# Moving normalisations, a bias and copies from VectorE to ScalarE and GpSimd in a twelve-sublayer perceiver kernel

## The chip, the core and the metric

The kernel runs on one core of one Trainium2 chip. The core has five engines that are spoken of here: TensorE (PE: matmuls, transposes, and its weight loads, PEld), VectorE (DVE), ScalarE (ACT), GpSimd (POOL), and the DMA queues that SyncE (SP) issues. Each engine carries out its own instructions in the order in which they stand in the built program, and waits for the others where data or buffers require it. The metric is device time in microseconds.

## The reference, cut to what matters

The model applies twelve residual sublayers to x of shape (128, 32, 128): four layers L0 to L3 of an xattn, an attn and an ffn each. Every sublayer reads a layer norm of x:

```python
x = x + _L1_xattn_ref(_layernorm(x), ctx_2048, ...)   # rmsnorm, one product, a depooled context
x = x + _L1_attn_ref(_layernorm(x), ...)              # a state-space block
x = x + _L1_ffn_ref(_layernorm(x), ...)               # 4 of 16 experts
x = x + _L2_xattn_ref(_layernorm(x), ctx_2048, ...)   # attention over 257 + 32 keys, 16 heads
x = x + _L2_attn_ref(_layernorm(x), ...)              # an RWKV recurrence and its channel mix
```

An expert of L1_ffn computes `min(h, 7) * sigmoid(1.702 * min(h, 7)) * 8` from `h = W1 x + b1`, then a second product. All arithmetic is in float32.

## The kernel before, in words

The 4096 tokens lie in SBUF as eight groups X[0] to X[7] of four tiles, each of 128 tokens by 128 channels. A layer runs group by group, and neighbouring layers are pipelined against each other:

- L0_xattn and then L0_ffn come first. The L1 layer of groups 0 and 1 runs as a side job in small steps between the experts of L0_ffn.
- `middle` (line 865) has nine iterations. Iteration `it` runs L2_xattn of group it, L1 (xattn13, L1_attn, L1_ffn) of group it + 2 and L2_attn of group it - 1. `abreast` interleaves the three by their steps: 20, 27 and 16. L1 takes part in iterations 0 to 5. Iterations 6 and 7 have L2_xattn and L2_attn alone, iteration 8 only the last L2_attn.
- L2_ffn follows, and then L3, in which xattn13 (line 947, shared by L1 and L3), L3_attn and L3_ffn run abreast.

The program does not fix an order for the engines except where `follow` does so: a scheduler of the framework takes the instructions as they are recorded and decides for each engine in which order they stand. Tiles come from pools; a tile with `bufs=2` has two buffers, and a new one waits until the old one has been read.

*Norms.* `stats` (line 189) computes mean and variance on DVE and takes the inverse root on POOL (line 215). `normed` (line 218) then applies (x - mean) * rs to each of four tiles on DVE (line 221). `normed_act` (line 1588), so far used only by L3_attn and L3_ffn, computes nb = -mean * rs on DVE (line 1592) and then rs * x + nb on ACT (line 1595). The result goes to `transposed` (line 228, PE) and from there into the first product.

*The experts of L1_ffn* (from line 1085). Each of 16 experts has a product ph (line 1087), DVE adds the bias and takes the minimum with 7 (line 1089, u), ACT takes a tanh (line 1091, s), DVE combines (line 1092, s), PE makes the second product py (line 1095), and four DVE instructions add it to X with the routing weight (line 827). PSUM tiles ph and py come from one pool of two buffers; u and s have two buffers each.

*L2_xattn.* A step handles one batch entry: POOL masks the query (QM, line 238, three buffers), PE makes four score tiles S (line 1180, two PSUM buffers), DVE takes the negated maximum nm (line 1181), ACT the exponential E (line 1182), PE transposes E in three key parts (line 1191, two PSUM buffers), these are copied to ET, the first and third part by ACT (line 1196) and the second by DVE (line 1194), and PE multiplies them with the values (line 1208), which ACT copies to OU (line 1209).

*L2_attn* has a norm of X twice over (xl and xn) and one of xl later on; kk (line 1298, POOL), xT, kv and exponentials on ACT, scans on DVE.

Of the kernel before, what the change touches and what calls it, by code (L numbers as in the profile page):

```python
# [9 lines left out]
FP = mybir.dt.float32  # L10
I32 = mybir.dt.int32
U32 = mybir.dt.uint32
AF = mybir.ActivationFunctionType
ALU = mybir.AluOpType
# [151 lines left out]
class Kern:  # L166
# [780 lines left out]
    def xattn13(self, g, w, hs, hps):  # L947
        nc = self.nc
        Dg = hs.tile([128, 4, 128], FP, tag="Dg")
        nc.sync.dma_start(Dg, self.dd[g * 512:(g + 1) * 512, :].rearrange("(i p) c -> p i c", p=128))  # L950
        mv, rs, s2 = self.stats(hs, self.X[g], 4, 1e-5, 1e-5)
        xn = self.normed(hs, self.X[g], mv, s2)
        pt = hps.tile([128, 512], FP, tag="m", name="pxt")
        self.transposed(pt, xn)
        xT = hs.tile([128, 512], FP, tag="xT")
        nc.scalar.activation(xT, pt, AF.Copy, scale=w["gres"])
        yield 1
        ps = hps.tile([128, 4, 128], FP, tag="m", name="ph")
        for i in range(4):
            nc.tensor.matmul(ps[:, i, :], lhsT=xT[:, i * 128:(i + 1) * 128], rhs=w["w"], start=True, stop=True)  # L960
        nc.gpsimd.tensor_tensor(Dg, Dg, w["ginit"].unsqueeze(1).to_broadcast([128, 4, 128]), ALU.mult)
        nc.gpsimd.tensor_tensor(Dg, Dg, w["b"].unsqueeze(1).to_broadcast([128, 4, 128]), ALU.add)
        nc.gpsimd.tensor_tensor(self.X[g], self.X[g], Dg, ALU.add)  # L963
        self.addx(g, ps.rearrange("p i c -> p (i c)"))
        yield 1
# [15 lines left out]
    def L1_attn(self, g, w, consts, ms, mps):  # L981
        nc = self.nc
        av, A, hw = consts
        wi = w["wi"].rearrange("p (k f) -> p k f", k=4)
        cw = hw[:, 0:8].rearrange("p (k j) -> p k j", k=2)
        dw, Bw, Cw = (w[n].rearrange("p (k s) -> p k s", k=2) for n in ("dw", "Bw", "Cw"))
        wo = w["wo"].rearrange("p (k d) -> p k d", k=2)
        mv, rs = self.stats(ms, self.X[g], 4, 1e-5)
        xn = self.normed(ms, self.X[g], mv, rs)
        ps = mps.tile([128, 512], FP, tag="m", name="pxt")  # L990
        self.transposed(ps, xn)
        xT = ms.tile([128, 512], FP, tag="xT")
        nc.scalar.copy(xT, ps)
        yield 1
        XC = ms.tile([128, 2, 16, T], FP, tag="XC")
        SG = ms.tile([128, 2, 512], FP, tag="SG")
        for k in range(2):
            ps = mps.tile([128, 16, T], FP, tag="m", name="pin")
            nc.tensor.matmul(ps, lhsT=wi[:, k, :], rhs=xT, start=True, stop=True)
            xc = XC[:, k]  # L1000
            nc.scalar.activation(xc, ps, AF.Identity, bias=hw[:, 8 + k:9 + k], scale=cw[:, k, 3:4])
            for j in (1, 2, 3):
                nc.vector.scalar_tensor_tensor(xc[:, :, j:], ps[:, :, :T - j], cw[:, k, 3 - j:4 - j], xc[:, :, j:], ALU.mult, ALU.add)
            yield 1
        XCf = XC.rearrange("p k b t -> p (k b t)")
        XS = ms.tile([128, 1024], FP, tag="XS")
        nc.scalar.activation(XS, XCf, AF.Tanh)
        nc.vector.scalar_tensor_tensor(XCf, XS, 1.0, XCf, ALU.add, ALU.mult)
        for k in range(2):
            ps = mps.tile([128, 512], FP, tag="m", name="pgt")  # L1010
            nc.tensor.matmul(ps, lhsT=wi[:, 2 + k, :], rhs=xT, start=True, stop=True)
            nc.scalar.activation(SG[:, k, :], ps, AF.Tanh, scale=0.5)
            nc.vector.scalar_tensor_tensor(SG[:, k, :], SG[:, k, :], 1.0, ps, ALU.add, ALU.mult)
        pd = mps.tile([128, 512], FP, tag="m", name="pd")
        for k in range(2):
            for j, lw in enumerate((dw[:, k, :], Bw[:, k, :], Cw[:, k, :], av)):
                nc.tensor.matmul(pd[32 * j:32 * j + 16], lhsT=lw, rhs=XC[:, k], start=k == 0, stop=k == 1)
        pB, pC, pX = pd[32:48], pd[64:80], pd[96:112]
        yield 1

        ze = ms.tile([128, 2, 512], FP, tag="XS", name="ze")
        z, e = ze[0:16, 0], ze[0:16, 1]
        nc.vector.tensor_scalar(z, pd[0:16], w["db"], None, ALU.add)
        nc.vector.scalar_tensor_tensor(e, z, -1.0, z, ALU.mult, ALU.min)
        nc.scalar.activation(e, e, AF.Exp)
        nc.scalar.activation(e, e, AF.Ln, bias=1.0)
        dt = z
        nc.vector.scalar_tensor_tensor(dt, z, 0.0, e, ALU.max, ALU.add)
        a = ms.tile([128, 16, T], FP, tag="xl", name="aa")[0:16]
        nc.scalar.activation(a.rearrange("p b t -> p (b t)"), dt, AF.Exp, scale=A)  # L1030
        nc.vector.memset(a[:, :, 0:1], 0.0)
        bx = ms.tile([128, 512], FP, tag="Dg", name="bx")[0:16]
        nc.vector.tensor_tensor(bx, dt, pX, ALU.mult)
        nc.vector.tensor_tensor(bx, bx, pB, ALU.mult)
        h = e
        nc.vector.tensor_tensor_scan(h, a.rearrange("p b t -> p (b t)"), bx, 0.0, ALU.mult, ALU.add)
        nc.vector.scalar_tensor_tensor(h, h, 0.5, pC, ALU.mult, ALU.mult)
        yield 1
        py = mps.tile([128, 512], FP, tag="m", name="py")
        nc.tensor.matmul(py, lhsT=self.ones[0:16, :], rhs=h, start=True, stop=True)  # L1040
        for k in range(2):
            nc.vector.tensor_tensor(SG[:, k, :], SG[:, k, :], py, ALU.mult)
            nc.vector.scalar_tensor_tensor(SG[:, k, :], XC[:, k].rearrange("p b t -> p (b t)"), w["D"][:, k:k + 1], SG[:, k, :], ALU.mult, ALU.add)
        po = mps.tile([128, 4, 128], FP, tag="m", name="po")
        for i in range(4):
            for k in range(2):
                nc.tensor.matmul(po[:, i, :], lhsT=SG[:, k, i * 128:(i + 1) * 128], rhs=wo[:, k, :], start=k == 0, stop=k == 1)
        self.addx(g, po.rearrange("p i c -> p (i c)"))
        yield 1
# [3 lines left out]
    def L1_ffn(self, g, w, gs, gps):  # L1053
        nc = self.nc
        w1 = w["w1"].rearrange("p (e i) -> p e i", e=16)
        w2 = w["w2"].rearrange("p (e d) -> p e d", e=16)
        mv, rs, s2 = self.stats(gs, self.X[g], 4, 1e-5, 1e-5)
        xn = self.normed(gs, self.X[g], mv, s2)
        ps = gps.tile([128, 512], FP, tag="m", name="pxt")
        self.transposed(ps, xn)  # L1060
        xT = gs.tile([128, 512], FP, tag="xT")
        nc.scalar.activation(xT, ps, AF.Copy, scale=w["sc"])
        yield 1
        xl = self.normed(gs, self.X[g], mv, rs, tag="xl")
        nc.gpsimd.tensor_tensor(self.X[g], self.X[g], xl, ALU.add)
        ps = gps.tile([128, 4, 16], FP, tag="m", name="plg")
        for i in range(4):
# [14 lines left out]
        self.addx(g, ps.rearrange("p i c -> p (i c)"))  # L1082
        nc.vector.tensor_scalar(R, R, 4.0, None, ALU.mult)
        yield 1
        for e in range(16):
            ps = gps.tile([128, 512], FP, tag="m", name="ph")
            nc.tensor.matmul(ps, lhsT=w1[:, e, :], rhs=xT, start=True, stop=True)
            u = gs.tile([128, 512], FP, tag="gu", bufs=2, name="u")
            nc.vector.tensor_scalar(u, ps, w["b1"][:, e:e + 1], 7.0, ALU.add, ALU.min)
            s = gs.tile([128, 512], FP, tag="gsw", bufs=2, name="s")  # L1090
            nc.scalar.activation(s, u, AF.Tanh, scale=0.851)
            nc.vector.scalar_tensor_tensor(s, s, 1.0, u, ALU.add, ALU.mult)
            py = gps.tile([128, 4, 128], FP, tag="m", name="py")
            for i in range(4):
                nc.tensor.matmul(py[:, i, :], lhsT=s[:, i * 128:(i + 1) * 128], rhs=w2[:, e, :], start=True, stop=True)
            self.add_weighted(self.X[g], py, R[:, :, e:e + 1])
            yield 1


# [10 lines left out]
    def L2_xattn(self, g, w, WP, e32, ys, yc, yx, yps, ypt, ypq):  # L1110
        nc = self.nc
        mv, rs = self.stats(ys, self.X[g], 4, 1e-5)
        xn = self.normed(ys, self.X[g], mv, rs)
        nc.gpsimd.tensor_tensor(self.X[g], self.X[g], w["bp"].unsqueeze(1).to_broadcast([128, 4, 128]), ALU.add)
        ps = ypq.tile([128, 512], FP, tag="q", name="pxt")
        self.transposed(ps, xn)
# [67 lines left out]
    def L2_xattn_transposes(self, st, t, b, cs, yx, ypt):  # L1184
        nc, E = self.nc, t["E"][b]
        for c in cs:
# [3 lines left out]
            for j in range(4):  # L1190
                self.follow(st, nc.tensor.transpose(pt[0:n, j * 128:(j + 1) * 128], E[:, j, k0:k1], self.ident))  # L1191
            ET = yx.tile([128, 512], FP, tag=f"ET{c}", name="ET")
            if c == 1:
                nc.vector.tensor_copy(ET[0:n], pt[0:n])  # L1194
            else:
                nc.scalar.copy(ET[0:n], pt[0:n])
            t["ET"][b].append(ET)

    def L2_xattn_values(self, st, t, b, yc, ypq):
# [41 lines left out]
    def L2_attn(self, g, w, wd, wt, wv, rs_, rpa):  # L1241
        nc = self.nc
        Wfv = wv.rearrange("p (k d) -> p k d", k=4)
        mv, rs, s2 = self.stats(rs_, self.X[g], 4, 1e-5, 1e-5)
        xl = self.normed(rs_, self.X[g], mv, rs, tag="xl")
        xn = self.normed(rs_, self.X[g], mv, s2)
        yield 1
        o = []
        for way in range(2):
# [33 lines left out]
        yield 1  # L1283

        mv, rs = self.stats(rs_, xl, 4, 1e-5)
        xn = self.normed(rs_, xl, mv, rs)
        ps = rpa.tile([128, 512], FP, tag="r", name="pxt2")
        self.transposed(ps, xn)
        xT = rs_.tile([128, 512], FP, tag="xT", name="xT2")
# [436 lines left out]
```

## Time and profile before

| what | us |
|---|---|
| median of 3 runs | 5026.24 (5025.77 to 5035.71) |
| the profiled execution | 5026.48 |
| its span, first to last instruction | 5024.7 |
| L1 of groups 0 and 1 beside L0_ffn | about 2200 to 2832 |
| iterations 0 to 5 of `middle` (with L1) | about 2832 to 3888 |
| iterations 6 and 7 | about 3888 to 4107 |
| last L2_attn | about 4107 to 4190 |
| L3 | about 4684 to the end |

The bounds are the first and last starts of the lines named: S of L2_xattn runs from 2832.5 to 4107.8, ph of L1_ffn ends at 3888, the first norm of L3_attn starts at 4684. The mean granted TensorE clock is 0.928 of full speed. A row of waits reads "engine, what it wanted to do, <- who released it: us in all, times, longest". A row of one line's instructions gives least, median and greatest duration in ns. Busy time of PE is that of pipelined matmuls, so a full row is not the peak of the engine.

### The profile page before, as it was taken

What the parts mean: (1) busy time and instruction counts of PE and PEld (TensorE: products, weight loads), DVE (VectorE), ACT (ScalarE), POOL (GpSimd) and SP (SyncE); (2) the same over time, 40 slices, a digit from 0 to 9 for tenths busy, and PEclk for the clock granted to TensorE, in tenths of its full rate; (3) what the DMA queues carried; (4) which work ended last, traced back from release to release, by engine and by line L of the source; (5) the groups of instructions that cost most, each with busy time, mean ns of one, the idle gap of its engine ahead of it and who ended that gap; (6) DMA issues with size and microseconds to landing.
All of it is one profiled execution on the core that took longest, in us unless ns stands there. A gap on an engine that the chain in (4) does not pass through costs nothing. (4 is left out here: it accounts for less than half of the span.)

```text
span 5024.7 us, 91248 instructions
## 1 busy us (share of the span) xinstructions
PE 4396.5 (87%) x34654; PEld 3147.0 (63%) x34654; DVE 3445.9 (69%) x10361; ACT 2388.4 (48%) x6481; POOL 1068.1 (21%) x1065
## 2 busy tenths in 40 slices
PE   7999898989898898879999888898888886879688
PEld 5777676767666676657766556565556653546455
DVE  5334959585867768582856689888888775777444
ACT  4555444454444445434444445454454554773233
POOL 1011111111111102121010122322322332322443
PEclk9999999999999999989999999999899987999677
DMA  4223141312222131323000001101010110000100
GB/s 138 61 60 56 43 67 38 63 47 56 47 54 53 49 60 41 51 74 40 1 12 3 27 27 28 28 26 29 25 28 28 37 42 19 1 1 14 38 13 11
DMA packets 354344, 193.27 MB, mean 38 GB/s; under 512 B 180065, under 2 KB 336481, under 8 KB 353265
## 3 DMA queue, kind: packets, MB, share of 16 engines
q1 hardware_dynamic: 353906, 187.45, 16.0%
q8 instruction: 273, 4.47, 0.4%
q14 instruction: 165, 1.35, 0.1%
HBM read 156.43 MB, written 30.96 MB: 37 GB/s over the span
## 5 line engine op out<-in xcount | busy, mean ns | idle before, releaser
L215 POOL TENSOR_TENSOR rs<-ve,w_const 128x4 f32<-128x4 f32 (+1 forms) x192 | 194.0, 1011 | 1706.2 <-DVE ve L213 1627.9
L541 PE MATMUL S<-cT,q 128*128 128x257 f32 x2048 | 535.4, 401 | 21.3 <-ACT E L545 21.0
L541 PEld LDWEIGHTS S<-cT,q 128*128 128x128 f32 x2048 | 386.6, 198 | 145.5 <-issue 57.8
L543 DVE TENSOR_REDUCE nm<-S 128x1 f32<-128x257 f32 x512 | 214.9, 420 | 367.5 <-PE S L541 365.7
L545 ACT ACTIVATE E<-S,nm 128x257 f32<-128x257 f32 x512 | 242.8, 475 | 362.3 <-DVE nm L544 361.3
L1180 PE MATMUL S<-cT,QM 128*128 128x289 f32 x1024 | 316.0, 427 | 74.7 <-ACT E L1182 69.8
L827 DVE SCALAR_TENSOR_TENSOR X<-py,R,X 128x128 f32<-128x128 f32 x768 | 223.6, 343 | 155.7 <-PE py L820 83.1
L1182 ACT ACTIVATE E<-S,nm 128x289 f32<-128x289 f32 x512 | 252.8, 498 | 153.6 <-DVE nm L1181 144.8
L820 PEld LDWEIGHTS py<-w_L_ffn,Hh 128*128 128x128 f32 x2048 | 259.6, 198 | 62.8 <-issue 40.3
L719 DVE TENSOR_TENSOR A<-A,elt 128x400 f32<-128x400 f32 (+22 forms) x608 | 295.6, 486 | 4.8
L524 PE MATMUL pq<-xT,WQK 128*128 128x128 f32 x2048 | 259.8, 284 | 36.1 <-ACT q L525 35.6
L717 DVE TENSOR_TENSOR elt<-A,row 128x400 f32<-128x400 f32 (+22 forms) x608 | 285.6, 470 | 8.0 <-DVE row L711 0.2
L580 PE MATMUL po<-TA,cN 128*128 128x512 f32 x512 | 274.9, 620 | 0.8 <-ACT TA L569 0.8
L1180 PEld LDWEIGHTS S<-cT,QM 128*128 128x128 f32 x1024 | 175.7, 194 | 158.5 <-issue 49.9
L524 PEld LDWEIGHTS pq<-xT,WQK 128*128 128x128 f32 x2048 | 244.8, 195 | 47.4 <-ACT q L525 43.7
L816 ACT ACTIVATE Hh<-pu,w_L_ffn 128x512 f32<-128x512 f32 x256 | 173.4, 686 | 212.6 <-PE pu L815 203.9
L820 PE MATMUL py<-w_L_ffn,Hh 128*128 128x128 f32 x2048 | 268.6, 284 | 3.7 <-ACT Hh L816 3.6
L581 PE MATMUL po<-TB,cN 128*128 128x512 f32 x512 | 267.6, 605 | 1.4 <-DVE TB L570 1.4
L555 ACT ACTIVATE E<-E,sm 128x256 f32<-128x256 f32 x512 | 218.4, 497 | 74.5 <-DVE sm L551 63.0
L815 PE MATMUL pu<-xT,w_L_ffn 128*128 128x512 f32 x512 | 247.6, 606 | 0.0
L1191 PE MATMUL pt<-w_const,E 128*96 128x128 f32 (+1 forms) x1536 | 233.2, 286 | 2.2 <-DVE ET L1194 1.9
L594 PE MATMUL pout<-WVO,OT 128*128 128x128 f32 x2048 | 234.2, 275 | 0.3 <-ACT OT L582 0.3
(471 smaller groups left out, 10204.7 us busy)
## 6 DMA issues: line engine op xcount, KB each, us to landing
cT<-ctxT SPq DMA_DIRECT2D x128, 257.0 KB
cN<-ctx SPq DMA_DIRECT2D x128, 256.0 KB
cT<-ctxT SPq DMA_DIRECT2D x32, 514.0 KB
phik<-PW SPq DMA_DIRECT2D x32, 256.0 KB
phiq<-P SPq DMA_DIRECT2D x32, 256.0 KB
A<-phik SPq DMA_DIRECT2D x128, 64.0 KB
PQ<-phiq SPq DMA_DIRECT2D x32, 256.0 KB
cN<-ctx SPq DMA_DIRECT2D x32, 194.0 KB
```

The costliest lines, as they stand in the source:

```text
L524: self.follow(st, nc.tensor.matmul(ps[:, k, :, :], lhsT=WQK[:, 4 * j + k, cb * 128:(cb + 1) * 128], rhs=t["x"], start=True, stop=True))
L541: self.follow(st, nc.tensor.matmul(S, lhsT=t["QP"][j][:, cb, b, :, :], rhs=t["cT"][b][:, cb, :], start=cb == 0, stop=cb == 1))
L545: nc.scalar.activation(E[:, j, 0:LK], S, AF.Exp, bias=m, accum_out=sm[:, j:j + 1])
L580: self.follow(st, nc.tensor.matmul(po, lhsT=cN[:, 0, c], rhs=TA, start=True, stop=False), nc.tensor.matmul(po, lhsT=cN[:, 1, c], rhs=TB, s ...
L581: nc.tensor.matmul(po, lhsT=cN[:, 1, c], rhs=TB, start=False, stop=True))
L594: self.follow(st, nc.tensor.matmul(po[:, 0, :], lhsT=OT[:, cb, h, :, :], rhs=WVO[:, cb, h, :], start=h == 0 and cb == 0, stop=False))
L717: nc.vector.tensor_tensor(t, A[:, k, :, i0:i1].rearrange("p h i -> p i h").unsqueeze(3).to_broadcast([128, m, HC, n]), row[:, :, i0:N].uns ...
L719: nc.vector.tensor_tensor(A[:, i0:i1, :, i0:N], A[:, i0:i1, :, i0:N], t, ALU.subtract)
L815: nc.tensor.matmul(ps, lhsT=wu[:, e, k * 128:(k + 1) * 128], rhs=xT[:, q, :], start=True, stop=True)
L820: nc.tensor.matmul(py[:, i, :], lhsT=Hh[k][:, i * 128:(i + 1) * 128], rhs=wd[:, e, k, :], start=k == 0, stop=k == 3)
L1180: self.follow(st, nc.tensor.matmul(S, lhsT=t["QM"][:, 0, 4 * j:4 * j + 4, :], rhs=t["cT"][:, b, :], start=True, stop=True))
L1182: nc.scalar.activation(E[:, j, :], S, AF.Exp, bias=nm[:, j:j + 1], accum_out=sm[:, j, b:b + 1])
```

## The change

Eight calls of `normed` become `normed_act`: in xattn13, in L1_attn, twice in L1_ffn, in L2_xattn, and three times in L2_attn. (xattn13's one call serves L1 and L3.) In L1_ffn the bias is added by ACT in reading ph out of PSUM, the minimum is taken in place by POOL, and the second product of an expert is recorded after the first product of the next, so that the loop has 17 steps. In L2_xattn the second transposed part is copied by ACT too. In the changed file the lines up to 1085 keep their numbers; bias, minimum, second product and tanh stand at 1091, 1092, 1097 and 1101, and what follows the loop stands seven lines further on, and four lines further on from the edit of the copies onward.

```diff
-        xn = self.normed(hs, self.X[g], mv, s2)
+        xn = self.normed_act(hs, self.X[g], mv, s2, "xn")
...
-        for e in range(16):
-            ps = gps.tile([128, 512], FP, tag="m", name="ph")
-            nc.tensor.matmul(ps, lhsT=w1[:, e, :], rhs=xT, start=True, stop=True)
-            u = gs.tile([128, 512], FP, tag="gu", bufs=2, name="u")
-            nc.vector.tensor_scalar(u, ps, w["b1"][:, e:e + 1], 7.0, ALU.add, ALU.min)
-            s = gs.tile([128, 512], FP, tag="gsw", bufs=2, name="s")
-            nc.scalar.activation(s, u, AF.Tanh, scale=0.851)
-            nc.vector.scalar_tensor_tensor(s, s, 1.0, u, ALU.add, ALU.mult)
-            py = gps.tile([128, 4, 128], FP, tag="m", name="py")
-            for i in range(4):
-                nc.tensor.matmul(py[:, i, :], lhsT=s[:, i * 128:(i + 1) * 128], rhs=w2[:, e, :], start=True, stop=True)
-            self.add_weighted(self.X[g], py, R[:, :, e:e + 1])
+        S = {}
+        for e in range(17):
+            if e < 16:
+                ps = gps.tile([128, 512], FP, tag="m", name="ph")
+                nc.tensor.matmul(ps, lhsT=w1[:, e, :], rhs=xT, start=True, stop=True)
+                u = gs.tile([128, 512], FP, tag="gu", bufs=2, name="u")
+                nc.scalar.activation(u, ps, AF.Identity, bias=w["b1"][:, e:e + 1])
+                nc.gpsimd.tensor_scalar(u, u, 7.0, None, ALU.min)
+            if e:
+                s = S.pop(e - 1)
+                py = gps.tile([128, 4, 128], FP, tag="m", name="py")
+                for i in range(4):
+                    nc.tensor.matmul(py[:, i, :], lhsT=s[:, i * 128:(i + 1) * 128], rhs=w2[:, e - 1, :], start=True, stop=True)
+                self.add_weighted(self.X[g], py, R[:, :, e - 1:e])
+            if e < 16:
+                s = gs.tile([128, 512], FP, tag="gsw", bufs=2, name="s")
+                nc.scalar.activation(s, u, AF.Tanh, scale=0.851)
+                nc.vector.scalar_tensor_tensor(s, s, 1.0, u, ALU.add, ALU.mult)
+                S[e] = s
             yield 1
...
-            if c == 1:
-                nc.vector.tensor_copy(ET[0:n], pt[0:n])
-            else:
-                nc.scalar.copy(ET[0:n], pt[0:n])
+            nc.scalar.copy(ET[0:n], pt[0:n])
...
-        xl = self.normed(rs_, self.X[g], mv, rs, tag="xl")
-        xn = self.normed(rs_, self.X[g], mv, s2)
+        xl = self.normed_act(rs_, self.X[g], mv, rs, "xl")
+        xn = self.normed_act(rs_, self.X[g], mv, s2, "xn")
```

More of the change, by code (lines that the diff above doesn't have):

```diff
@@ L988, in L1_attn @@
         mv, rs = self.stats(ms, self.X[g], 4, 1e-5)
-        xn = self.normed(ms, self.X[g], mv, rs)
+        xn = self.normed_act(ms, self.X[g], mv, rs, "xn")
         ps = mps.tile([128, 512], FP, tag="m", name="pxt")
@@ L1057, in L1_ffn @@
         mv, rs, s2 = self.stats(gs, self.X[g], 4, 1e-5, 1e-5)
-        xn = self.normed(gs, self.X[g], mv, s2)
+        xn = self.normed_act(gs, self.X[g], mv, s2, "xn")
         ps = gps.tile([128, 512], FP, tag="m", name="pxt")
@@ L1063, in L1_ffn @@
         yield 1
-        xl = self.normed(gs, self.X[g], mv, rs, tag="xl")
+        xl = self.normed_act(gs, self.X[g], mv, rs, "xl")
         nc.gpsimd.tensor_tensor(self.X[g], self.X[g], xl, ALU.add)
@@ L1112, in L2_xattn @@
         mv, rs = self.stats(ys, self.X[g], 4, 1e-5)
-        xn = self.normed(ys, self.X[g], mv, rs)
+        xn = self.normed_act(ys, self.X[g], mv, rs, "xn")
         nc.gpsimd.tensor_tensor(self.X[g], self.X[g], w["bp"].unsqueeze(1).to_broadcast([128, 4, 128]), ALU.add)
@@ L1285, in L2_attn @@
         mv, rs = self.stats(rs_, xl, 4, 1e-5)
-        xn = self.normed(rs_, xl, mv, rs)
+        xn = self.normed_act(rs_, xl, mv, rs, "xn")
         ps = rpa.tile([128, 512], FP, tag="r", name="pxt2")
```

## The prediction

> **What bounds the kernel now.** First the page: TensorE (PE) is busy 87% of the span, VectorE (DVE) 69%, ScalarE (ACT) 48%, GpSimd (POOL) 21%. The slices show where DVE is fullest, the three after the middle; that is where L1, L2_xattn and L2_attn run abreast.
>
> ```profile
> PE 4396.5 (87%) x34654; PEld 3147.0 (63%) x34654; DVE 3445.9 (69%) x10361; ACT 2388.4 (48%) x6481; POOL 1068.1 (21%) x1065
> DVE  5334959585867768582856689888888775777444
> ```
>
> Second, the windows view, cut by what runs: L1 of groups 0 and 1 beside L0_ffn; six iterations with an L1 in them; two of L2_xattn and L2_attn alone; L3. Columns: length, then busy time of PE, PEld, DVE, ACT, POOL, then clock.
>
> ```profile
> 2200.00:2832.00 632.00, 602.80 (x4104) 432.41 (x4104) 397.62 (x1362) 262.62 (x414) 61.97 (x56) 0.97 0.09 14
> 2832.00:3888.00 1056.00, 919.17 (x6811) 630.59 (x6809) 895.45 (x2235) 517.92 (x1370) 290.53 (x276) 0.95 0.10 28
> 3888.00:4107.00 219.00, 190.61 (x1672) 137.56 (x1671) 163.95 (x326) 129.25 (x386) 73.37 (x72) 0.97 0.11 31
> ```
>
> PE idles 29 us in the first, 137 in the second, 28 in the third; nothing larger can be won there while PE's work stays as it is. In the second DVE is 85% busy, ACT 49%. Third, whom PE waited for in the six iterations (us, times, longest), and then the same for ACT:
>
> ```profile
> PE S L1180 <- ACT E L1182: 49.7, 45, 2.3
> PE py L1095 <- DVE s L1092: 27.7, 32, 2.1
> PE pxt L228 <- DVE xn L221: 21.3, 13, 2.3
> PE po L1047 <- DVE SG L1043: 8.8, 5, 2.2
> ```
>
> ```profile
> ACT s L1091 <- DVE u L1089: 114.3, 68, 5.5
> ACT E L1182 <- DVE nm L1181: 91.6, 90, 3.6
> ```
>
> So ACT, whose exponentials free the buffers of S, itself stands waiting for DVE's maxima (nm): DVE's queue is what PE feels. In the two L2 iterations PE loses 20.1 us to S.
>
> Fourth, the rows that price the edits (ns: least, median, most):
>
> ```profile
> L221 DVE TENSOR_SCALAR xn<-X,mv,s x128: 251/340/1149, 2256.8 to 4936.1; 128x128 f32<-128x128 f32 x128
> L1595 ACT ACTIVATE xn<-X,nb,rs x64: 477/478/493, 4684.2 to 5009.4; 128x128 f32<-128x128 f32 x64
> L1592 DVE SCALAR_TENSOR_TENSOR nb<-mv,rs x16: 155/163/1219, 4684.0 to 5008.0; 128x4 f32<-128x4 f32 x16
> L1089 DVE TENSOR_SCALAR u<-ph,w_L_ffn x128: 717/742/752, 2632.6 to 3888.9; 128x512 f32<-128x512 f32 x128
> L816 ACT ACTIVATE Hh<-pu,w_L_ffn x256: 668/687/699, 2178.6 to 2809.5; 128x512 f32<-128x512 f32 x128
> L1194 DVE COPY ET<-pt x128: 620/680/689, 2842.7 to 4111.5; 96x512 f32<-96x512 f32 x128
> L1238 POOL TENSOR_SCALAR wv<-w_L_attn x1: 1495/1495/1495, 2559.7 to 2559.7; 128x512 f32<-128x512 f32 x1
> ```
>
> **The change, part by part.** The built programs confirm the counts: ACT +545 instructions (one an extra table load, 1.28 us), DVE -472, POOL +128, PE unchanged.
>
> *Norms.* 72 calls (16 of xattn13, half of them in L3; 8 L1_attn, 16 L1_ffn, 8 L2_xattn, 24 L2_attn). Each drops 4 x 0.340 = 1.36 us of DVE, adds 0.163 us of DVE (nb) and 4 x 0.478 = 1.91 us of ACT, and one more hand-over. On the path to the transposes it is about 0.7 us longer (0.16 + 0.55).
>
> *Bias and minimum.* 128 experts drop 0.742 us of DVE; ACT gets a biased pass from PSUM, like the row L816, 0.687 us; POOL gets the minimum. For that there is one row of the same operation and shape, 1.495 us, but a single sample. The Trainium skill (GPSIMD Engine Reference, § 4.1 Engine selection and § 3.1) sends elementwise work to VectorE and calls one-input GpSimd work roughly line-rate, 1.03 cycles per element at 1.2 GHz: 512 elements 0.44 us, about 0.6 with dispatch, an estimate. By the rule the step from ph to s is 0.69 + 0.6 + 0.63 + 0.69 = 2.6 us plus four hand-overs, some 3.4; by the row 3.5 plus these, 4.3. I take the row and keep 0.6 for the range.
>
> *Third transpose tile.* 128 copies move: DVE -0.680, ACT about +0.58 (its row for the other two tiles has a median of 582 ns).
>
> *Loads per iteration.* With an L1 (8 norms, 16 experts, 16 tiles; length 176): DVE 149.2 - 10.9 + 1.3 - 11.9 - 10.9 = 117 (66%); ACT 86.3 + 15.3 + 11.0 + 9.3 = 122 (69%); POOL 48.4 + 24 = 72 (41%). L2 alone (4 norms, 16 tiles; length 109.5): DVE 82 - 5.4 + 0.7 - 10.9 = 66 (61%), ACT 64.6 + 7.7 + 9.3 = 82 (74%). PE stays at 153 and 95, so it remains the fullest engine.
>
> The skill also speaks against this half (ScalarE: Activation LUTs, § Rules for kernel authors: add, multiply and minimum belong on VectorE). The norm rows agree on the price: ACT loses 288 x 0.138 = 40 us more than DVE saves. If instruction time set the end, the norms would cost up to 40 us; but neither engine sets it, so I count only the wait they lengthen.
>
> *S.* Its wait runs through nm (DVE) and E (ACT). As a rough measure of queueing I take busy/(1 - busy), an assumption: with L1 5.6 + 1.0 before, 2.0 + 2.2 after, a ratio of 0.65, so 49.7 becomes 32, -17 us. For L2 alone 3.0 + 1.4 before, 1.6 + 2.9 after: no change, 0 (bounds -5 and +15, since all copies of a step now stand in one queue with E).
>
> *One expert behind.* In the built orders I summed the PE work between an expert's ph and its py, at the trace's paces. Before, it is 3.2 us on average in the middle; a chain of 2.75 us (seen from 3336.61 to 3339.36) overruns it for 29 of 96 experts, 14 us in all, beside the 32 waits and 27.7 us measured. After, it is 6.1 us; a chain of 4.3 overruns it 15 times, by 6.7 us. Scaled by 27.7/14 that is 13: -14 us. With the rule's POOL price hardly an overrun is left: -27.
>
> *What the new wait holds up.* tanh stands on ACT behind u and now waits for POOL. Behind it stand E, ET, OU. In the built order 33 of the 96 pairs are adjacent; the work between averages 0.56 us against some 1.7 to be bridged: a stall of 1.1 us, and DVE's u costs 114.3/96 = 1.2 now. I count 0. POOL's queue can add to it: 59 of 96 minima have something other than a minimum directly ahead (19 times QM, which can itself wait for S).
>
> *Norms on the path.* PE waited for xn 13 times in the six iterations: 13 x 0.7 = +9, less some 4 because rs and nb come sooner from a shorter DVE queue: +5. Beside L0_ffn +3 (PE waited 6 times for xn there, some four of these 0.7 longer), L3 +4 (8 norms), the L2_attn alone at the end +2. po on DVE's SG: 8.8 becomes 6, -3. The extra twenty-eighth step of L1 issues nothing but the last py: 0. No DMA moves on its queue.
>
> Sum: -17 - 14 + 5 - 3 + 0 + 3 + 4 + 2 = -20. The profiled execution took 5026.48 (span 5024.7 and 1.8 around it), 0.2 above the median of 5026.24: 5026 - 20 = 5006.
>
> **The rivals.**
>
> *A. PE fills up.* Beside L0_ffn, with DVE at 63%, PE is busy 95%. If DVE was the only brake, the six iterations go to 93%: 919/0.93 = 988, -68, and the rest +9: 4967. For it: DVE is named in nearly every wait. Against: the S chain with two buffers stays, and in the L2 iterations PE is at 87% with DVE at 75%.
>
> *B. POOL's minimum stops ACT: slower.* Place: tanh in ACT's queue, E behind it, S behind E. If the minimum waits behind QM, kk or rs (1.04 us each, or QM's own wait for S), the stall grows by 1.0 us or more for 59 experts and by 0.5 for the others: 59 x 1.2 + 37 x 0.5 = 90 us of ACT. With half of it reaching PE, +45; the gain at py is lost too (+14): -20 + 45 + 14 = +39, 5065. It decides once the wait of tanh averages above 1.2 + 2 x 20/96 = 1.6 us. For it: POOL is strictly in order and its QM idles 391 us in the middle waiting for S. Against: the order of the queues puts minima together where S is far off.
>
> *C. Waits change their name only.* S then waits for ACT's queue as long as it did for DVE's, py's gain pays for the norms: 5026 within 10.
>
> **How the numbers follow.** About 0.2% (10 us) is what a measurement can tell from no change. Forecast (4980 to 5016) 0.35, A 0.15, C 0.18, B 0.32. Faster 0.50, same 0.18, slower 0.32. The range takes in most of A and of B and the cheap POOL price, 4955 to 5065; what is left out is some 0.2. The forecast's own range is 4980 to 5016.
>
> **What would show it.** Right: in the stage with L1, PE's wait for s nearly gone or below 15 us, its wait for E near 32, ACT near 69% busy, DVE near 66%, the minimum at 1.0 to 1.5 us; L2 iterations as long as before. Wrong: ACT's wait for POOL's u well over 150 us with PE's wait for E above 60 (B); the minimum far over 1.5 us; L2 iterations longer than 115 us; PE above 92% (A).

## The result, and the profile after

| what | before | after |
|---|---|---|
| median of 22 runs, us | 5029.38 (5022.67 to 5046.29) | 5043.64 (5025.96 to 5050.09) |
| the profiled execution, us | 5026.48 | 5031.06 |
| its span, us | 5024.7 | 5029.3 |

The ratio is 1.0020, with an interval of 1.0013 to 1.0027: the change made the kernel slower, by some 10 us (the medians lie 14 apart, the means 10). The forecast was 5006. The profiled execution of after is the third quickest of its 22, and its L3 is the shortest in all profiles here; the stages ahead of L3 show the loss.

The table cuts both spans at the same events: the first product of L0_ffn, the first S of L2_xattn, the last S ("the middle"), the first S of L2_ffn and the first S of L3_attn. The two kernels with which the cause is shown below stand beside them (all from profiles, us).

| kernel | L1 beside L0_ffn | middle | to L2_ffn | L2_ffn | L3 |
|---|---|---|---|---|---|
| before | 655.9 | 1275.3 | 104.0 | 481.6 | 331.3 |
| after | 670.0 | 1275.7 | 102.6 | 480.6 | 321.8 |
| after without its minimum | 657.1 | 1206.6 | 102.5 | 480.1 | 333.1 |
| after with the minimum twice | 697.0 | 1392.7 | 103.3 | 480.3 | 327.9 |

So 14 us were lost beside L0_ffn and nothing was won in the middle. Each row is one profile, and L3 is no evidence: in the twelve other kernels here that share after's edits to L3's code it took from 323.3 to 333.1, in the five with before's L3 from 331.3 to 334.9.

The work moved as planned. First the page of after, busy time and DVE's and ACT's slices:

```profile
PE 4403.0 (88%) x34654; PEld 3145.0 (63%) x34654; DVE 3224.6 (64%) x9889; ACT 2640.6 (53%) x7026; POOL 1271.2 (25%) x1193
...
DVE  5334949595867768582855467667766655877444
ACT  4555444454444445434445556666666663773343
```

DVE's full stretch is gone: the eight slices from the 24th on, where the middle lies, read 8 and 9 in before (the prediction speaks of three) and 6 and 7 here. Then the windows of after, L1 beside L0_ffn, the six iterations with an L1 (they start 16 us later than before), and the two with L2 alone:

```profile
2200.00:2832.00 632.00, 599.61 (x4076) 431.60 (x4074) 363.13 (x1294) 293.40 (x472) 94.48 (x74) 0.96 0.08 12
2848.00:3904.00 1056.00, 918.94 (x6792) 627.29 (x6792) 734.13 (x1899) 688.73 (x1746) 448.82 (x375) 0.95 0.10 28
3904.00:4124.00 220.00, 196.58 (x1677) 137.14 (x1677) 140.30 (x276) 153.47 (x441) 75.08 (x75) 0.98 0.11 31
```

In the six iterations DVE fell from 85% to 70%, ACT rose from 49% to 65%, POOL from 28% to 43%, and the iterations are as long as they were. Whom PE waited for in them, in after:

```profile
PE S L1187 <- ACT E L1189: 41.1, 45, 3.0
PE pxt L228 <- ACT xn L1599: 18.0, 10, 3.5
PE py L1097 <- DVE s L1102: 14.6, 16, 1.8
PE py L1097 <- DVE X L827: 9.5, 10, 1.8
PE S L1187 <- POOL rs L215: 9.0, 4, 3.0
PE prt L834 <- DVE R L859: 8.4, 5, 2.5
```

The two waits that the change aimed at are shorter (49.7 to 41.1, 27.7 to 14.6), but the last three, which before did not have in the middle, make up 27 us. And for ACT in the same stretch:

```profile
ACT s L1101 <- POOL u L1092: 121.6, 96, 3.1
ACT E L1189 <- DVE nm L1188: 89.6, 102, 3.5
...
ACT xn L1599 <- DVE nb L1596: 33.3, 32, 2.5
ACT u L1091 <- PE ph L1089: 33.1, 45, 2.4
```

The first line is the important one: all 96 tanhs stand waiting for GpSimd, 1.27 us each. It looks like before's line for s and u (114.3), and that likeness is what misled the forecast. Last the rows of the moved work in after:

```profile
L1091 ACT ACTIVATE u<-ph,w_L_ffn x128: 666/687/702, 2637.3 to 3901.5; 128x512 f32<-128x512 f32 x128
...
L1092 POOL TENSOR_SCALAR u<-u x128: 1485/1486/1808, 2638.1 to 3902.3; 128x512 f32<-128x512 f32 x128
...
L1599 ACT ACTIVATE xn<-X,nb,rs x192: 477/480/518, 2577.3 to 5013.9; 128x128 f32<-128x128 f32 x192
```

### The profile page after: what moved, and what is told of

It reads as the page before. It is cut to its first block, busy times and chain, and to the rows that moved or that the text cites. A ratio compares the mean times of both kernels' runs of the same rounds, so it can differ in the third digit from the quotient of the medians.

```text
span 5029.3 us, 91615 instructions
## 1 busy us (share of the span) xinstructions
PE 4403.0 (88%) x34654; PEld 3145.0 (63%) x34654; DVE 3224.6 (64%) x9889; ACT 2640.6 (53%) x7026; POOL 1271.2 (25%) x1193
## 5 line engine op out<-in xcount | busy, mean ns | idle before, releaser
L541 PE MATMUL S<-cT,q 128*128 128x257 f32 x2048 | 534.8, 401 | 20.4 <-ACT E L545 20.1
L1187 PE MATMUL S<-cT,QM 128*128 128x289 f32 x1024 | 337.0, 443 | 71.1 <-ACT E L1189 53.7
L1188 DVE TENSOR_REDUCE nm<-S 128x1 f32<-128x289 f32 x512 | 224.2, 450 | 100.8 <-PE S L1187 96.3
L1092 POOL TENSOR_SCALAR u<-u 128x512 f32<-128x512 f32 x128 | 192.3, 1502 | 295.8 <-ACT u L1091 249.1
```

The source lines that it names most:

```text
L541: self.follow(st, nc.tensor.matmul(S, lhsT=t["QP"][j][:, cb, b, :, :], rhs=t["cT"][b][:, cb, :], start=cb == 0, stop=cb == 1))
L1187: self.follow(st, nc.tensor.matmul(S, lhsT=t["QM"][:, 0, 4 * j:4 * j + 4, :], rhs=t["cT"][:, b, :], start=True, stop=True))
L1188: nc.vector.tensor_reduce(nm[:, j:j + 1], S, AX.X, ALU.max, negate=True)
```

## The experiments

The theory: the minimum on GpSimd, directly in front of the tanh in ACT's strictly ordered queue, takes back what the other edits win. In its first form (T1 below) it sought the loss beside L0_ffn alone and gave the other parts little weight. Its rivals: the norms on ACT cost it; the order "one expert behind" costs it; the third copy fills ACT; or GpSimd has too much work, wherever the minimum stands.

Every ratio is to before, measured in the same batch; microseconds are the ratio's distance from 1 times 5030. By the intervals such a figure is uncertain by 5 to 10 us, and a difference of two by up to 13. The mean granted clock of a kernel's runs lies between 0.924 and 0.929, but for norms alone (0.932) and the minimum twice (0.918). Among before's own runs beside these two, 0.01 of clock goes with 16 and with 23 us, so some 9 us of the first and 16 of the second may go with the clock; nothing here separates that from the edit.

**Each part alone, on before.** Only the eight calls of the norms:

```diff
-        xn = self.normed(hs, self.X[g], mv, s2)
+        xn = self.normed_act(hs, self.X[g], mv, s2, "xn")
```

> Only the eight norm calls on ScalarE; experts and tile copies as before. Stage = first pu of L0_ffn to first S of L2_xattn: 656 us before, 670 changed. Theory T1 (the loss is ScalarE's queue beside L0_ffn: the expert's tanh waits there for GpSimd and holds the gelus up): stage within 4 us of 656, total within 5 us of before. Rival T2 (norms cost their longer hand-over everywhere, in the middle too): total +8 to +15 us, PE waiting over 25 us for xn in the middle. Rival T3 (the one-behind loop spoils the hand-over to the middle): no change here, total 0.

Measured: 4988.65, ratio 0.9912 (0.9899 to 0.9925), -44 us, which none of the three theories had. The norms on ACT are a gain, although each costs ACT 0.48 us where it cost DVE 0.34.

Only the loop of the experts, the whole of that edit:

```diff
-            nc.vector.tensor_scalar(u, ps, w["b1"][:, e:e + 1], 7.0, ALU.add, ALU.min)
+                nc.scalar.activation(u, ps, AF.Identity, bias=w["b1"][:, e:e + 1])
+                nc.gpsimd.tensor_scalar(u, u, 7.0, None, ALU.min)
...
+            if e:
+                s = S.pop(e - 1)
```

> Only the expert loop (bias on ScalarE, minimum on GpSimd, second product one expert behind). T1: the stage beside L0_ffn 8 to 14 us longer than 656, and the middle 5 to 15 us shorter since the wait for s falls from 28 to about 15 us; total 0 to +8. T2: total -10 or better, the loss being the norms'. T3: stage 10 to 15 us longer, from the steps after the last product of L0_ffn alone.

Measured: 5051.45, ratio 1.0036 (1.0023 to 1.0048), +18 us; 11 of them beside L0_ffn (666.6 there) and 10 in the middle (1285.0), where T1 had a gain. The loss is in this edit.

Only the copies:

```diff
-            if c == 1:
-                nc.vector.tensor_copy(ET[0:n], pt[0:n])
-            else:
-                nc.scalar.copy(ET[0:n], pt[0:n])
+            nc.scalar.copy(ET[0:n], pt[0:n])
```

> Only the second transposed tile copied by ScalarE. T1 and T3: stage beside L0_ffn unchanged at 656; middle (first S to last S, 1275 us) within 6 us; total within 6 us. T2 (ScalarE becomes the queue that S waits for in the L2 iterations): middle +10 us or more, PE's wait for E above 75 us where it was 70.

Measured: 5003.5, ratio 0.9941 (0.9925 to 0.9956), -30 us, where at most 6 were expected. Alone they pay as well.

Only the order: second product one expert behind, bias and minimum left on DVE:

```diff
-            nc.scalar.activation(s, u, AF.Tanh, scale=0.851)
+            if e:
+                s = S.pop(e - 1)
+                py = gps.tile([128, 4, 128], FP, tag="m", name="py")
...
+            if e < 16:
+                s = gs.tile([128, 512], FP, tag="gsw", bufs=2, name="s")
+                nc.scalar.activation(s, u, AF.Tanh, scale=0.851)
```

> Only the order: second product one expert behind, bias and minimum still in one VectorE instruction. T1: stage beside L0_ffn within 4 us of 656, since ScalarE waits for nothing new; the middle 10 to 20 us shorter, PE's wait for s below 8 us from 28; total -10 to -20. T3: stage +10 to +15 us, total 0 or slower. T2: total -10 to -20 as T1.

Measured: 4996.81, ratio 0.9921 (0.9906 to 0.9936), -40 us, more than expected. Within the loop it is therefore not the order that loses. What is left of it is bias and minimum: the step from -40 to +18.

**Bias and minimum, on after.** Both back on DVE:

```diff
-                nc.scalar.activation(u, ps, AF.Identity, bias=w["b1"][:, e:e + 1])
-                nc.gpsimd.tensor_scalar(u, u, 7.0, None, ALU.min)
+                nc.vector.tensor_scalar(u, ps, w["b1"][:, e:e + 1], 7.0, ALU.add, ALU.min)
```

> The changed kernel with one part undone: bias and minimum again in one VectorE instruction; norms, tile copies and the order of the second product as changed. Runs so far against before: norms -44 us, tile copies -30, order alone -36, experts with ScalarE and GpSimd +18. Theory H (the minimum on GpSimd makes ScalarE stand at the tanh): total -70 to -110, stage beside L0_ffn near 658, middle 1180 to 1205. Rival X (the parts do not add up: once ScalarE carries norms and copies, it is the bound): total -20 to -50 only.

Measured: 4991.24, ratio 0.9910 (0.9895 to 0.9926), -45 us. This is short of what the theory said and in the range of its rival X: the other parts do not add up. Bias and minimum as changed cost 55 us on top of them (from -45 to +10). The tanh waits less for DVE here than in before, where the same stretch has 116.4:

```profile
ACT s L1100 <- DVE u L1091: 69.6, 55, 2.9
```

No minimum at all (the experts then compute with h where the reference takes min(h, 7)):

```diff
-                nc.gpsimd.tensor_scalar(u, u, 7.0, None, ALU.min)
```

> The changed kernel without the minimum: the expert computes with h instead of min(h, 7), so GpSimd has nothing to do for it and the tanh can follow its bias at once. H: nearly as fast as with VectorE doing both, total -60 to -110. Rival L (the 0.69 us per expert of ScalarE's busy time is what costs, 88 us in all): within 15 us of the changed kernel, total 0 to +15.

Measured: 4957.51, ratio 0.9850 (0.9836 to 0.9863), -75 us. From 1.0020 to 0.9850 is 85 us, or 0.67 us for each of 128 minima of 1.49. In the profiles 13 of it lie beside L0_ffn and 69 in the middle. Where the 69 are is best seen with the weight loads (PEld): their busy time in the middle is nearly the same in both kernels (764.6 and 762.3), so what is lost stands in their waits. In after, between the first and last S (2848.6 to 4124.3):

```profile
PEld S L1187 <- ACT E L1189: 75.7, 147, 2.6
...
PEld py L1097 <- DVE s L1102: 22.3, 22, 2.7
PEld pt L1198 <- ACT ET L1200: 16.2, 37, 1.2
...
PEld py L1097 <- DVE X L827: 15.2, 11, 2.7
```

and without the minimum (2830.5 to 4037.1):

```profile
PEld S L1186 <- ACT E L1188: 63.9, 131, 2.6
...
PEld pt L1197 <- ACT ET L1199: 9.0, 32, 0.5
...
PEld py L1096 <- DVE s L1101: 6.6, 9, 1.9
PEld py L1096 <- DVE X L827: 6.2, 9, 1.2
```

All waits of the weight loads there add up to 463 us in after and 395 without the minimum, 68 apart; with equal busy time that sum has to fit, and what the lines tell is who was waited for. No single wait carries it: s gives 15.7, E 11.8, X 9.0, ET 7.2, and smaller ones the rest. This is as it should be if an in-order queue stands still. All that stands behind the tanh on ACT comes a little later (E, ET), DVE in turn stands for s (22.8 us without the minimum; the line of after is below), and what is behind that in DVE's queue (X) is late too:

```profile
DVE s L1102 <- ACT s L1101: 70.3, 64, 2.2
```

Two other causes can be looked for in the traces. The scheduler might have built other queues: in the middle, POOL's order is the same but for 7 of 348 instructions besides the minimum, but 162 of ACT's 2185 and 192 of DVE's 2176 stand elsewhere, so a part of the 85 may be order. And GpSimd's work might lengthen DVE's own instructions: 87 of them in after's middle take over 0.1 us more than the median of their kind, 52 us in all; without the minimum 70 do, 44 us in all. That leaves some 8 us for this cause.

The same minimum on DVE, in SBUF, with the bias still on ACT:

```diff
-                nc.gpsimd.tensor_scalar(u, u, 7.0, None, ALU.min)
+                nc.vector.tensor_scalar(u, u, 7.0, None, ALU.min)
```

> The changed kernel with the minimum on VectorE, in SBUF, behind ScalarE's bias: the hand-over between two engines stays, but it is short and GpSimd keeps only what it had. H in its form of a 1.49 us instruction: total -40 to -90, ScalarE's wait for u under 70 us. Rival R (any engine between bias and tanh stops ScalarE as long): ScalarE's wait for u stays above 100 us and the total within 15 us of the changed kernel.

Measured: 4972.27, ratio 0.9875 (0.9860 to 0.9890), -63 us. Its row, and what ACT waits for it between the first and last S:

```profile
L1092 DVE TENSOR_SCALAR u<-u x128: 403/426/1235, 2637.8 to 3835.2; 128x512 f32<-128x512 f32 x128
```

```profile
ACT s L1101 <- DVE u L1092: 22.7, 37, 0.9
```

The minimum costs some 12 us here against 85 on GpSimd, and the wait of the tanh is a fifth of after's. With the minimum on DVE, the bias on ACT is worth 18 (from -45 to -63).

**GpSimd's work or the place in front of the tanh?** All 128 minima stay on GpSimd, but the tanh and all after it come one step later, so that a whole step lies between minimum and tanh:

```diff
-            if e:
-                s = S.pop(e - 1)
+                U[e] = u
+            if e > 1:
+                s = S.pop(e - 2)
...
-            if e < 16:
+            if 0 < e < 17:
+                u = U.pop(e - 1)
```

> The changed kernel with the tanh and what follows recorded one expert later, so that a bias of the next expert stands between bias and tanh; the minimum stays on GpSimd. H: ScalarE's wait for GpSimd falls from 161 us to under 60, total -40 to -80. Rival Q (GpSimd's own queue is the cost: the minimum's 190 us hold up QM and the inverse roots): the wait at the tanh falls, but the total stays within 15 us of the changed kernel and PE's waits on GpSimd stay above 12 us.

Measured: 4981.66, ratio 0.9891 (0.9876 to 0.9906), -55 us. With as much work for GpSimd as in after, 65 of the 85 us come back. PE's waits on GpSimd in the middle stayed (16.8 us, 14.5 in after), as the rival had it, but the total did not. ACT's wait between the first and last S shrank less than expected, though:

```profile
ACT s L1103 <- POOL u L1092: 79.3, 65, 3.5
```

The middle takes 1214.1, close to the 1206.6 without a minimum. Beside L0_ffn nothing came back (676.2).

The same question from the other side: a second minimum behind the first.

```diff
                 nc.gpsimd.tensor_scalar(u, u, 7.0, None, ALU.min)
+                nc.gpsimd.tensor_scalar(u, u, 7.0, None, ALU.min)
```

> The changed kernel with the minimum taken twice in a row on GpSimd, the same result. H: ScalarE stands 1.4 us longer per expert, 128 x 1.4 = 180 us in all; with about half reaching PE as from no minimum (-75) to one (+10), +60 to +110 more, total +70 to +120. If the loss is only a matter of the order in which the queues were built: within 25 us of the changed kernel.

Measured: 5181.93, ratio 1.0298 (1.0279 to 1.0318), +150 us, so 140 more than after and more than expected: 1.1 us for each 1.49 us of GpSimd. ACT's wait and DVE's wait for ACT in the middle:

```profile
ACT s L1102 <- POOL u L1093: 221.8, 98, 5.1
```

```profile
DVE s L1103 <- ACT s L1102: 146.2, 89, 4.3
```

Both grew along with it (from 121.6 and 70.3). The first minimum costs 45% of its duration, the second 74%, as if what slack there is had gone into the first. Five kernels have norms, copies and order in common and differ only in bias and minimum; set side by side, the total follows the wait at the tanh:

| bias and minimum | wait of the tanh in the middle, us | total against before, us |
|---|---|---|
| bias on ACT, no minimum | 0 | -75 |
| bias on ACT, minimum on DVE | 22.7 | -63 |
| both in one DVE instruction | 69.6 | -45 |
| bias on ACT, minimum on GpSimd | 121.6 | +10 |
| bias on ACT, minimum twice on GpSimd | 221.8 | +150 |

Now the kernels that keep GpSimd's work and take the tanh out of its way in other forms. The tanh reads u before the minimum, which is written to another tile, so that only the combination waits for GpSimd (a tanh of 0.851 h differs from that of 0.851 min(h, 7) by about 1e-5 at most):

```diff
-                nc.gpsimd.tensor_scalar(u, u, 7.0, None, ALU.min)
+                v = V[:, e % 2, :]
+                nc.gpsimd.tensor_scalar(v, u, 7.0, None, ALU.min)
...
-                nc.vector.scalar_tensor_tensor(s, s, 1.0, u, ALU.add, ALU.mult)
+                nc.vector.scalar_tensor_tensor(s, s, 1.0, V[:, e % 2, :], ALU.add, ALU.mult)
```

> The changed kernel, but the tanh reads u before the minimum (tanh(0.851 h) for h over 7 differs by some 1e-5), and GpSimd writes the minimum to another tile, which only VectorE's product reads. GpSimd does the same 128 instructions, ScalarE the same work; only ScalarE's wait for GpSimd is gone. H: -55 to -80 against before, like the kernel without a minimum (-75). Rival Q (GpSimd's queue, or its chain to the second product): no better than -25, PE's wait for s above 12 us.

Measured: 4999.27, ratio 0.9934 (0.9917 to 0.9951), -33 us: half of the 85 come back, less than expected. ACT no longer waits for GpSimd; instead DVE stands in front of the combination:

```profile
DVE s L1104 <- POOL V L1094: 57.8, 60, 2.5
```

The same form with the minimum on DVE:

```diff
+                v = V[:, e % 2, :]
+                nc.vector.tensor_scalar(v, u, 7.0, None, ALU.min)
```

> The best guess: as the one with the tanh unclipped, but the minimum on VectorE (0.43 us in SBUF), off ScalarE's way. H: -65 to -85, the 0.43 us on VectorE costing little; about 5 us better or worse than the minimum on GpSimd off the way.

Measured: 4968.24, ratio 0.9867 (0.9848 to 0.9886), -66 us, which cannot be told from the simpler form (0.9875). With the minimum on DVE it makes no measurable difference whether the tanh waits for it.

Then the tanh ahead of a minimum on GpSimd once more, and the combination one step later still:

```diff
             if e < 16:
-                s = gs.tile([128, 512], FP, tag="gsw", bufs=2, name="s")
+                U[e] = s = Y[e // 2 % 2][:, e % 2, :]
                 nc.scalar.activation(s, u, AF.Tanh, scale=0.851)
-                nc.vector.scalar_tensor_tensor(s, s, 1.0, u, ALU.add, ALU.mult)
+            if 0 < e < 17:
+                S[e - 1] = s = U.pop(e - 1)
+                nc.vector.scalar_tensor_tensor(s, s, 1.0, V[:, (e - 1) % 2, :], ALU.add, ALU.mult)
```

> As the kernel with the tanh unclipped and the minimum on GpSimd, but VectorE's product, which reads the minimum, recorded one expert later, so that no queue reads it at once. The same 128 minima on GpSimd. Theory H in its general form (the price is the wait of the queue that reads the minimum next): -55 to -80 against before, VectorE's wait for GpSimd's V under 40 us. Rival Q (GpSimd's load itself): no better than the -33 us of the unclipped one.

Measured: 4983.33, ratio 0.9904 (0.9889 to 0.9918), -48 us, with a middle of 1221.9. It is better than with the combination in the same step (-33), and short of what was expected. DVE still stands for GpSimd even with a step between:

```profile
DVE Y L1106 <- POOL V L1094: 62.9, 56, 2.7
```

So the place explains half to three quarters of the 85 us, not all. Three kernels with unchanged work for GpSimd regain 65, 43 and 58 us. From 20 to 42 us of the 85 stay as long as the minimum is on GpSimd, and beside L0_ffn a step of distance brings nothing. What makes up this rest is open.

**Do the gains add up?** Alone, norms, copies and order bring 44 + 30 + 40 = 114, together (with DVE's minimum) 45. Norms and copies on before, with the old loop:

```diff
+        xn = self.normed_act(hs, self.X[g], mv, s2, "xn")
...
+            nc.scalar.copy(ET[0:n], pt[0:n])
```

> Norms and tile copies on ScalarE, experts as before (one VectorE instruction, second product in the same step). Alone they gave -44 and -30 us. If the parts add up: -65 to -80. If they share one gain, VectorE's relief for S: -35 to -55, about what both with the changed order gave (-45).

Measured: 5014.71, ratio 0.9962 (0.9951 to 0.9973), -19 us, less than either alone. PE's wait for the exponentials in its middle:

```profile
PE S L1180 <- ACT E L1182: 94.6, 67, 6.2
```

It was 69.8 in before's, 81.0 with the norms alone and 37.5 with the copies alone. That suggested that the copies take from the whole once the norms are on ACT. To test it: after with the minimum on DVE, and the copies put back:

```diff
-            nc.scalar.copy(ET[0:n], pt[0:n])
+            if c == 1:
+                nc.vector.tensor_copy(ET[0:n], pt[0:n])
+            else:
+                nc.scalar.copy(ET[0:n], pt[0:n])
```

> Norms, bias on ScalarE, minimum on VectorE, one expert behind, but the second transposed tile copied by VectorE as before. With the copies this gave -63 us. If the copies take from the whole once ScalarE has the norms: -75 to -100. If VectorE's relief is what pays: -35 to -50.

Measured: 4988.11, ratio 0.9908 (0.9892 to 0.9924), -46 us. With the copies it was -63, so they pay 17 there: that theory fell. And with the norms back on DVE as well, so that of the change only the loop is left, its minimum on DVE (these lines are against after):

```diff
-        xn = self.normed_act(hs, self.X[g], mv, s2, "xn")
+        xn = self.normed(hs, self.X[g], mv, s2)
...
-                nc.gpsimd.tensor_scalar(u, u, 7.0, None, ALU.min)
+                nc.vector.tensor_scalar(u, u, 7.0, None, ALU.min)
```

> Only the expert loop as changed, with the minimum on VectorE. The same loop with GpSimd's minimum gave +18 us, the order alone -39. H: -35 to -60. If the bias pass on ScalarE were what cost: 0 to +18.

Measured: 5001.56, ratio 0.9945 (0.9925 to 0.9964), -28 us, less than expected, and no better than the order alone (-40): without norms and copies on ACT, the bias on ACT does not pay. This gives a ladder from before to after, each step on top of the one ahead of it:

| step | us |
|---|---|
| loop with bias on ACT, minimum on DVE, one expert behind | -28 |
| norms on ACT | -18 |
| third copy on ACT | -17 |
| the minimum from DVE to GpSimd | +73 |
| sum | +10 |

By itself, without norms and copies, the last step costs 46 (from -28 to +18). It is dearer in after, where ACT has more to do; that more then stands behind each tanh is a likely reason, not a shown one. Why the copies lose 25 on top of the norms in the old loop and win 17 in the new one stays open: with every edit the scheduler builds other orders of the queues, and no run here separates that from the load.

**The loss beside L0_ffn.** After, with the old loop for groups 0 and 1 alone:

```diff
+        if g < 2:
+            for e in range(16):
...
+                nc.vector.tensor_scalar(u, ps, w["b1"][:, e:e + 1], 7.0, ALU.add, ALU.min)
...
+            return
```

> The changed kernel, but groups 0 and 1, whose L1 runs beside L0_ffn, use the old expert loop. If the expert loop makes the loss there: stage from the first pu to the first S at 656 within 5 us, total -2 to -14. If the norms or chance make it: stage 665 to 672, total within 6 us of the changed kernel.

Measured: 5024.75, ratio 0.9981 (0.9970 to 0.9992), -10 us, 20 better than after, as expected. The stage beside L0_ffn takes 653.1 instead of 670.0, the middle 1282.8. With the norms on ACT and the old loop the stage takes 653.0 elsewhere too (norms alone; norms and copies). So the new loop costs 17 us there, and 13 of them are the minimum's (657.1 without it).

The best version of the runs is after with the minimum on DVE, 0.9875 of before (or 0.9867 with the tanh ahead of it): it keeps every other edit, and is 1.4% faster than after.

## Why the prediction was wrong, point by point

- *The prices.* They held. The minimum: a single row of 1.495 was taken over the Trainium skill's line rate (some 0.6, an estimate from GPSIMD Engine Reference, § 3.1), and 128 of them measure 1.486: two and a half times that estimate. Bias 0.687 as put; norm 0.480 for 0.478; nb 0.162 for 0.163; copy 0.584 for 0.58.
- *The loads.* DVE 70% for 66%, ACT 65% for 69%, POOL 43% for 41% in the six iterations, and PE stayed the fullest. Loads were right, and said nothing on the end.
- *One expert behind, 27.7 to 13.* Measured 14.6. The wait came out as put; the order alone, as a part, is worth 40 us and not 14.
- *S, 49.7 to 32.* Measured 41.1: half of the gain. The ratio of busy/(1 - busy) knows how full ACT is and not that it stands still. In the L2 iterations 20.1 became 12.6 where no change was put.
- *"What the new wait holds up": this is the step that failed.* Its estimate of the new wait was good: 1.1 us per tanh were put, 1.27 came. But from "DVE's u costs 114.3/96 = 1.2 now" it took the sum of 0. The runs put +55 in its place. The kernel with all other edits and DVE's u takes -45, where the other terms had -20, and the new bias and minimum bring it to +10. The comparison was with a wait of before, which the other edits would have shortened anyway (116.4 to 69.6 us in the middle). And a wait that stays equally long is not free: without any wait at the tanh the change is worth -75, and the minimum takes 85 of it. What should have been asked is what the kernel would take without either wait.
- *The other terms* come to +3 beside L0_ffn, where 14 were lost, 13 of them the minimum's; +5 for the norms, whose wait fell a little (21.3 to 19.0 in the middle), while norms alone are worth -44; -3 for SG, whose wait fell from 8.8 to 1.8; +4 in L3 and +2 at the end, neither of which the stages show. Three waits that the sum did not have, X 9.5, rs 9.0 and R 8.4, take 27 us of PE in the six iterations. The first is the minimum's for the most part (1.5 without it). The other two are not (10.5 and 11.3 without it): they come with the other edits.
- *The rivals.* A (4967) is near to what the change does without its minimum (0.9850, or 4955). B named the mechanism and the place that the runs show: tanh in ACT's queue, E behind it. It was too small in its price (59 against 85), and its threshold was wrong: it should decide from 1.6 us per tanh, and did at 1.27, because it too counted only what came on top of the old wait. Its loss was to be taken from 20 us, and was taken from 75, so that +39 became +10. C's total fits the middle (1275.3 and 1275.7), by accident: not because waits only changed their names, but by a gain of 69 us and a loss of as much.

## What to carry to other kernels

When a wait in a strictly ordered queue is replaced by another of the same length, don't book it at nothing: price the kernel without either, since that is what the change gives away. An engine with time to spare was a poor place here for a step that stands directly ahead of an instruction on a fuller engine: its latency made up more of the price than its load, and a step of distance in the program gave half to three quarters back. Test a change of several parts by its parts, and then in company: here three parts that gain 30 to 44 us each alone, and 45 together, hid one that loses 73.

## What was not expected of the hardware

- The same minimum over 128x512 in SBUF takes 1.486 us on GpSimd and 0.426 on DVE; from PSUM with a bias DVE took 0.742. Splitting the step so that ACT empties PSUM and DVE works in SBUF was worth 18 us with norms and copies on ACT, and cost 12 without them, which is at the edge of the noise.
- PE's own waits show only 48 of the 69 us that the minimum costs the middle (157.0 and 109.2 in sum). The rest is in a PE that is busy for 22 us longer (1115.8 and 1094.3) with the same matmuls, so PE's idle time is no fixed measure of what can be won.
- All 87 lengthened DVE instructions of after's middle, and all 70 without the minimum, ran while GpSimd was busy too. GpSimd is busy for 41% of the one and 31% of the other.
